# Where the products of a two-step graph walk stand: factoring x U1 + R (x U1') out of the first step

## The chip, the core and the metric

The kernel runs on one core of one Trainium2 chip. The metric is device time in microseconds (us) of one execution. The core's engines are called PE (matrix products), PEld (its weight loads), DVE (vector), ACT (scalar), POOL (GpSimd) and SP (which here issues DMAs).

## The reference

x has 2708 rows of 256 numbers, adj is a sparse 2708 x 2708 matrix. Layer 0 walks twice over two matrices and adds up terms; layer 1 is a graph attention over adj. Cut to what the change touches:

```
R = adj + I;  R = R / R.sum(-1)
Xf = X;  Xa = X;  Z = 0
for n in range(2):
    A  = top_p_attention(Xa)        # softmax of a bilinear form, smallest 10% dropped, rows sum to 1
    Xf = R @ Xf
    Xa = A @ Xa
    Z  = Z + Xf @ U1[n].T + Xa @ U2[n].T
h = X + Z
x = layernorm(x + (layernorm(h) * ln_g + ln_b))
x = layernorm(x + gat(x, adj))      # layer 1
```

The walk's part of Z is R x U1[0].T + R R x U1[1].T. It does not depend on the attention's part, apart from the sum.

## The kernel before, in words

The 2708 rows are cut into 22 tiles: 16 of 128 rows and 6 of 110. All products are in float32; one product shows as two records in the trace.

For each step s and tile t there are two streams of work. **The search** (`scores`, `survey`, `bound`, `candidates`, `settle`) computes a tile of exponentials e, 128 x 2708, finds the threshold of the top 90% and sets the rest to zero. It uses PE for the scores (L620), ACT for exponentials (L624) and, in step 1, four passes over e (L645), DVE for maxima (L725, L743), replacing (L745, L791) and masked products (L710, L794), and POOL for small numbers. **The attention product** (`weigh`) transposes e in six groups (L202), ACT copies each to SBUF as eT (L208), and PE multiplies 22 times (L217) with the values x (step 0) or ba (step 1). A search is begun three tiles ahead.

**The walk** is the third stream, a generator `walks()`. For s = 0 tile t takes 22 products (L845) of blocks of adj transposed (`blk`, loaded by SP into three buffers, two loads a tile) with xe, which is x with a column of ones; the sum lands in a PSUM tile `walk` of a pool with one buffer. `after_walk0` adds the tile's own row on DVE (xf, L858), takes the reciprocal of the row sum, transposes xf on PE (L603), and `terms1` multiplies by U1 of both steps at once (L890). ACT scales the two halves by the reciprocal: cs is the contribution of step 0, and yw = (R x) U1[1].T is the operand of the second walk. POOL adds the own row's share and x to cs (L900 to L902) and stores it in DRAM as c1. For s = 1 the walk multiplies with yw; `finish` scales the result on ACT (xw, L924), adds c1, c2 (the attention's share of step 0, from `terms2`, L910) and the attention of step 1 (`held`), makes both layer norms and calls `sources`, which prepares layer 1.

The order on PE, ACT, DVE and POOL is written out by hand, as the program emits it. `slot(spend)` moves every running search by one piece, then every running follow-up (`doing`), then emits `spend` walk products, fewer where a walk tile ends. A slot follows each of the six groups of an attention tile; the tuples SPEND_0 and SPEND_1 give its walk products. Ahead of step 0 there are ten slots (SPEND_FIRST), between the steps some sixteen (SPEND_BETWEEN). The second walk can't start before the last `after_walk0` is through (`unfinished`). SP's queue and the pools' buffers are ordered by the framework.

```
SPEND_FIRST, SPEND_0 = 5, (2, 2, 2, 2, 2, 1)
SPEND_BETWEEN, SPEND_1 = 6, (5, 5, 4, 5, 5, 4)
```

Of the kernel before, what the change touches and what calls it, by code (L numbers as in the profile page):

```python
# [8 lines left out]
F32 = mybir.dt.float32  # L9
BF16 = mybir.dt.bfloat16  # L10
I32 = mybir.dt.int32
AF = mybir.ActivationFunctionType
ALU = mybir.AluOpType
# [3 lines left out]
P = 128  # L17
# [3 lines left out]
CHUNK = 512  # L21
# [12 lines left out]
NARROW = 26.0  # L34


SPEND_FIRST, SPEND_0 = 5, (2, 2, 2, 2, 2, 1)
SPEND_BETWEEN, SPEND_1 = 6, (5, 5, 4, 5, 5, 4)
HELD = 8
LN2 = 0.6931471805599453  # L40

Z_LOW, Z_HIGH = 1e-25, 1e30
# [3 lines left out]
def kernel(  # L46
# [16 lines left out]
    nc = tc.nc  # L63
    N, D = x.shape
# [50 lines left out]
    vd = [kept.tile([P, D], F32, name=f"v_{t}") for t in range(NT)]  # L115
    bad = const.tile([1, 1], I32, name="bad")

    def load_x():
        step = 4
        for t0 in range(0, NT, step):  # L120
            by_tile(xe[:, t0:, 0:D], x, t0, min(t0 + step, NT))

    def layernorm(dst, src, m):

# [100 lines left out]
    def general_layer0():  # L225
        with ExitStack() as l0:
# [5 lines left out]
            u_sb = w0.tile([P, STEPS, 2, DC, D], F32, name="u_sb")  # L232
            g_sb = w0.tile([P, D], F32, name="g_sb")
            b_sb = w0.tile([P, D], F32, name="b_sb")
            load_x()
            nc.scalar.dma_start(w1_sb, w1T.rearrange("(c p) e -> p c e", p=P))
            nc.scalar.dma_start(w3_sb, w3T.rearrange("(c p) e -> p c e", p=P))
            for s in range(STEPS):
# [245 lines left out]
    def fast_layer0(ep, adjp):  # L484
# [32 lines left out]
            nc.scalar.dma_start(w2_sb[:, h, :], w2T)  # L517
        for h in range(2):
            nc.scalar.dma_start(wk_sb[:, :, h, :], w3T.rearrange("(c p) e -> p c e", p=P))
        load_x()  # L520
        for s in range(STEPS):
            for k, u in enumerate((u1T, u2T)):
                nc.scalar.dma_start(u_sb[:, k, :, s], u[s].rearrange("(c p) e -> p c e", p=P))
# [27 lines left out]
        nc.gpsimd.memset(wants, 0.0)  # L551
        nc.gpsimd.memset(haves, 0.0)

        yw = keep.tile([P, NT, D], F32, name="yw")
        ba = keep.tile([P, NT, D], F32, name="ba")
        rinv = keep.tile([P, NT], F32, name="rinv")
        qT = keep.tile([P, N], F32, name="qT")
# [1 line left out]
        dram = l0.enter_context(tc.tile_pool(name="dram", bufs=1, space=bass.MemoryType.DRAM))  # L559
        c1 = [dram.tile([P, D], F32, name=f"c1_{t}") for t in range(NT)]  # L560
        c2 = [dram.tile([P, D], F32, name=f"c2_{t}") for t in range(NT)]


        kT = [wk.tile([P, HN], F32, name="junk"), keep.tile([P, HN], F32, name="kT1")]
# [248 lines left out]
        def walks():  # L813

            queue = [
                (s, t, j0, j1)
                for s in range(STEPS) for t in range(NT) for j0, j1 in ((0, HT), (HT, NT))  # L820
            ]

            def load(s, t, j0, j1):
                m = rows[t]
                blk = adjp.tile([P, NT - HT, P], F32, name="blk")
                by_tile(blk[:, :, :m], adjT[:, off[t] : off[t + 1]], j0, j1)
                return blk

            ahead = load(*queue[0])
            for n, (s, t, j0, j1) in enumerate(queue):  # L830
                m = rows[t]
                cur, w = (xe, D + 1) if s == 0 else (yw, D)
                while s and unfinished:
                    yield True
                blk = ahead
                if n + 1 < len(queue):
                    ahead = load(*queue[n + 1])
                if j0 == 0:
                    ac = ps_wk.tile([P, CHUNK], F32, name="walk")
                    if s:  # L840
                        ca, cb = (finp.tile([P, D], F32, name=k) for k in ("ca", "cb"))
                        nc.sync.dma_start(ca[:m], c1[t][:m])
                        nc.sync.dma_start(cb[:m], c2[t][:m])
                for j in range(j0, j1):
                    nc.tensor.matmul(  # L845
                        ac[:m, :w], blk[: rows[j], j - j0, :m], cur[: rows[j], j, 0:w],
                        start=(j == 0), stop=(j == NT - 1),
                    )
                    if j == NT - 1:
                        doing.append(after_walk0(t, ac) if s == 0 else finish(t, ac, ca, cb))  # L850
                        next(doing[-1])
                    yield j == NT - 1

        def after_walk0(t, ac):
            m = rows[t]
            unfinished.add(t)
            xf = rowp.tile([P, D + 1], F32, name="xf")
            nc.vector.tensor_add(xf[:m], ac[:m, : D + 1], xe[:m, t, :])  # L858
            nc.vector.reciprocal(rinv[:m, t : t + 1], xf[:m, D : D + 1])
            yield  # L860
            tp = ps_tr.tile([P, 4, P], F32, name="tr")
            xT = turn(xf, m, tp, nc.scalar.copy)
            yield
            terms1(t, xT)
            unfinished.remove(t)

        pair = []
# [17 lines left out]
        def terms1(t, xT):  # L885

            m = rows[t]
            cy = ps_tr.tile([P, 4, P], F32, name="tr").rearrange("p a b -> p (a b)")
            for c in range(DC):
                nc.tensor.matmul(  # L890
                    cy[:m], xT[:, c, :m], u_sb[:, 0, c].rearrange("p s e -> p (s e)"),
                    start=(c == 0), stop=(c == DC - 1),
                )
            r = rinv[:m, t : t + 1]
            cs = rowp.tile([P, D], F32, name="cs")
            nc.scalar.activation(cs[:m], cy[:m, 0:D], AF.Copy, scale=r)
            nc.scalar.activation(yw[:m, t, :], cy[:m, D : 2 * D], AF.Copy, scale=r)

            own = rowp.tile([P, D], F32, name="own", bufs=1)
            nc.gpsimd.tensor_scalar(own[:m], yw[:m, t, :], r, None, op0=ALU.mult)  # L900
            nc.gpsimd.tensor_add(cs[:m], cs[:m], own[:m])
            nc.gpsimd.tensor_add(cs[:m], cs[:m], xe[:m, t, 0:D])  # L902
            nc.gpsimd.dma_start(c1[t][:m], cs[:m])

        def terms2(t, xT):
# [13 lines left out]
        def finish(t, ac, ca, cb):  # L919

            m = rows[t]
            xt = xe[:m, t, 0:D]
            xw = rowp.tile([P, D], F32, name="xw")[:m]
            nc.scalar.activation(xw, ac[:m, :D], AF.Copy, scale=rinv[:m, t : t + 1])  # L924
            yield
            while t not in held:
                yield
            hh = heldp.tile([P, D], F32, name="hh", bufs=4)[:m]
            nc.gpsimd.tensor_add(ca[:m], ca[:m], cb[:m])
            nc.gpsimd.tensor_add(ca[:m], ca[:m], held.pop(t)[:m])  # L930
            nc.gpsimd.tensor_add(hh, ca[:m], xw)
            yield
            for last in range(2):
                st, mv = small.tile([P, 6], F32, name="ln_st")[:m], small.tile([P, 2], F32, name="ln_mv")[:m]
                nc.vector.bn_stats(st, hh)
                nc.vector.bn_aggr(mv, st)
                yield
                yield
                ve, rs = new("ln_ve", m), new("ln_rs", m)
                nc.gpsimd.tensor_scalar(ve, mv[:, 1:2], LN_EPS, None, op0=ALU.add)  # L940
                nc.gpsimd.tensor_tensor(rs, ve, minus_half[:m], op=ALU.pow)
                yield
                yield
                nc.vector.tensor_scalar(
                    xt if last else hh, hh, mv[:, 0:1], rs, op0=ALU.subtract, op1=ALU.mult
                )
                yield
                yield
                if not last:
                    nc.gpsimd.tensor_mul(hh, hh, g_sb[:m])  # L950
                    nc.gpsimd.tensor_add(hh, hh, b_sb[:m])
                    nc.gpsimd.tensor_add(hh, hh, xt)
                    yield
                    yield
            yield from sources(t, rowp, ps_tr)


        engines = {nc.tensor.engine, nc.scalar.engine, nc.vector.engine, nc.gpsimd.engine}
        going, doing, unfinished = [], [], set()
        ready, held = {}, {}  # L960
        stream = walks()
        owed = [0]
# [30 lines left out]
        def step(s, cur, spend):  # L993
            for t in range(NT):
# [6 lines left out]
                def between(n):  # L1001
                    last = n == len(groups) - 1
                    if last:
                        xa = heldp.tile([P, D], F32, name="xa1")
                        nc.scalar.activation(xa[:m], ac[:m, :D], AF.Copy, scale=rden)
                        if s:
                            held[t] = xa
                        else:
                            doing.append(after_attention0(t, xa))
                    slot(spend[n], (s, t + 3) if last else None)  # L1010
# [25 lines left out]
                    )  # L1036


        for grp in groups:
            k = rows[grp[0]]  # L1040
            w, c0 = k * len(grp), off[grp[0]]
            tp = ps_lg.tile([P, 2, CHUNK], F32, name="lg")
            for c in range(DC):
                for q, t in enumerate(grp):
                    nc.tensor.transpose(
                        tp[:, c, q * k : (q + 1) * k], xe[:k, t, c * P : (c + 1) * P],
                        ident[:k, :k],
                    )
            e = ep.tile([P, N], F32, name="e")
            xT = e[:, 0 : DC * CHUNK].rearrange("p (c n) -> p c n", c=DC)  # L1050
            nc.scalar.copy(xT[:, 0, :w], tp[:, 0, :w])
            nc.vector.tensor_copy(xT[:, 1, :w], tp[:, 1, :w])
            pj = ps_lg.tile([P, 2, CHUNK], F32, name="lg")
            for n, wm in enumerate((wq, wk_sb)):
                for c in range(DC):
# [5 lines left out]
            keep_k(0, c0, w, pj[:, 1], nc.vector.tensor_copy)  # L1061
        with tc.manual_schedule(engines=engines):
            for n in range(10):
                slot(SPEND_FIRST if n else 0, (0, n // 4) if n in (0, 4, 9) else None)
            layer1_weights()
            step(0, xe, SPEND_0)
            while doing:
                slot(SPEND_BETWEEN)

# [242 lines left out]
```

## Time and profile before

| what | value |
|---|---|
| median of 3 runs | 1678.13 us (1677.03 to 1678.82) |
| the profiled execution | 1677.58 us, span 1675.8 us |
| PE busy | 1610.0 us, 96% of the span |
| PEld, DVE, ACT, POOL busy | 1058.0, 1217.0, 766.8, 423.4 us |
| walk products with xe, with yw (L845) | 240.5 and 228.1 us |
| attention products with x, with ba (L217) | 233.3 and 234.1 us |
| transposes of e (L202) | 140.8 us |
| U1 products (L890), transposes of xf (L603) | 42.9 and 9.1 us |

Busy times of PE overlap with each other, since products are pipelined. In the lines of the trace the form is start, duration, engine, line, operation, out<-in and, in brackets, the idle time of the engine before it with what ended it; in the chain of waits it is start, duration, engine, tile and line.

### The profile page before, as it was taken

The page shows a single profiled execution, that of the slowest core. Times are in us where ns is not written, and L with a number is a line of the kernel's source. Part 1 is how long each engine was busy: PE and PEld are TensorE (multiplying, and loading weights), DVE is VectorE, ACT ScalarE, POOL GpSimd, SP SyncE. Part 2 cuts the span into 40 slices and gives each one's busy share as a digit, 9 for nine tenths or more (in the row PEclk, how much of TensorE's full clock was granted, in tenths as well). Part 3 has the DMA queues.
Part 4 walks back from the last instruction along what each step waited for, and adds up shares of the span by engine and source line. Part 5 has one row for each costly group of instructions (what it writes and reads, how often), then busy time and mean ns, then how long its engine had stood idle before and what let it go on. Part 6 is the DMA issues. An engine that isn't in the chain of part 4 may idle for free.

```text
span 1675.8 us, 23985 instructions
## 1 busy us (share of the span) xinstructions
PE 1610.0 (96%) x8218; PEld 1058.0 (63%) x8218; DVE 1217.0 (73%) x3660; ACT 766.8 (46%) x1324; POOL 423.4 (25%) x893
## 2 busy tenths in 40 slices
PE   7999999999999999999999999999997999999895
PEld 4677777777777776777787878777785222322332
DVE  2954554565455019888999999998994899888886
ACT  1333333333333255656576666667555334243231
POOL 0310111111011023223244444444434020420313
PEclk9999999999999999999999999999999999999998
DMA  6211011111110142212322322323222332232231
GB/s 166 73 47 46 26 43 40 40 31 40 40 43 25 43 104 67 63 49 73 79 72 79 87 68 82 89 58 77 72 65 88 98 99 86 88 93 77 76 86 39
DMA packets 153873, 113.89 MB, mean 68 GB/s; under 512 B 39898, under 2 KB 144094, under 8 KB 153742
## 3 DMA queue, kind: packets, MB, share of 16 engines
q1 hardware_dynamic: 149278, 105.18, 23.4%
q0 software_dynamic: 2112, 5.55, 1.0%
q10 hardware_dynamic: 2352, 1.54, 0.3%
q8 instruction: 67, 1.10, 0.3%
q14 instruction: 64, 0.52, 0.1%
HBM read 101.16 MB, written 11.09 MB: 67 GB/s over the span
## 4 chain that ended last, share of the span: by engine, by line
PE 78%; DVE 9%; ACT 5%; POOL 4%; issue 3%; DMA 0%; ACTq 0%; POOLq 0%; DVEq 0%; SPq 0%
PE att L217 23%; PE walk L845 19%; PE acc L1233 12%; PE acc L1240 6%; PE lg L620 5%; PE tr L202 4%; ACT e L624 3%; PE tr L910 2%; PE tr L890 2%; PE lg L1056 1%; PE tr L591 1%; DVE cand L725 1%; ACT eT L208 1%; DVE scr L791 1%; POOL res L1192 1%
## 5 line engine op out<-in xcount | busy, mean ns | idle before, releaser
L645 ACT ACTIVATE junk<-e,minus,rth 128x2708 bf16<-128x2708 f32 (+1 forms) x88 | 232.8, 2646 | 35.7 <-POOL rth L677 34.6
L845 PE MATMUL walk<-xe,blk 128*128 128x257 f32 (+3 forms) x968 | 240.5, 382 | 0.0
L217 PE MATMUL att<-ba,eT 128*128 128x256 f32 (+3 forms) x968 | 234.1, 383 | 5.0 <-ACT eT L208 5.0
L217 PE MATMUL att<-xe,eT 128*128 128x256 f32 (+3 forms) x968 | 233.3, 381 | 4.3 <-ACT eT L208 4.3
L208 ACT COPY eT<-tr 128x512 f32<-128x512 f32 (+5 forms) x264 | 138.2, 537 | 206.3 <-PE tr L202 206.1
L1233 PE MATMUL acc<-pt,v 128*64 128x512 f32 (+3 forms) x1056 | 226.0, 550 | 4.7 <-DVE pt L1225 3.8
L845 PE MATMUL walk<-yw,blk 128*128 128x256 f32 (+3 forms) x968 | 228.1, 381 | 1.7 <-ACT xw L924 1.7
L725 DVE MAX8 cand<-e 128x8 f32<-128x170 f32 (+1 forms) x352 | 89.2, 322 | 178.8 <-ACT e L624 178.8
L845 PEld LDWEIGHTS walk<-xe,blk 128*128 128x128 f32 (+3 forms) x968 | 174.6, 186 | 54.2 <-issue 29.3
L845 PEld LDWEIGHTS walk<-yw,blk 128*128 128x128 f32 (+3 forms) x968 | 176.7, 186 | 41.5 <-issue 11.5
L1225 DVE SCALAR_TENSOR_TENSOR pt<-e,tj,blk 128x1024 f32<-128x1024 f32 (+3 forms) x176 | 185.8, 1115 | 19.8 <-issue 8.0
L217 PEld LDWEIGHTS att<-ba,eT 128*128 128x128 f32 (+3 forms) x968 | 171.4, 186 | 32.7 <-ACT eT L208 10.0
L217 PEld LDWEIGHTS att<-xe,eT 128*128 128x128 f32 (+3 forms) x968 | 170.9, 186 | 30.9 <-ACT eT L208 7.2
L624 ACT ACTIVATE e<-lg 128x1024 f32<-128x1024 f32 (+1 forms) x132 | 121.1, 921 | 132.3 <-PE lg L620 132.3
L1233 PEld LDWEIGHTS acc<-pt,v 128*64 128x64 f32 (+1 forms) x1056 | 72.1, 137 | 153.5 <-issue 112.3
L202 PE MATMUL tr<-ident,e 128*128 128x128 f32 (+3 forms) x968 | 140.8, 270 | 4.6 <-ACT xT L606 3.8
L202 PEld LDWEIGHTS tr<-ident,e 128*128 128x128 f32 (+3 forms) x968 | 115.1, 139 | 32.3 <-ACT xT L606 6.1
L1165 ACT ACTIVATE blk<-blk 128x1024 f32<-128x1024 f32 (+3 forms) x66 | 63.2, 958 | 155.3 <-DMA blk<-in_adjT_dram 136.3
L1240 PE MATMUL acc<-pt,sb 128*32 128x512 f32 (+3 forms) x1056 | 124.5, 549 | 0.0
L1225 DVE SCALAR_TENSOR_TENSOR pt<-r,tj,blk 128x1024 f32<-128x1024 f32 (+1 forms) x88 | 109.8, 1306 | 10.8 <-issue 7.0
L631 POOL TENSOR_TENSOR fact<-zp 128x1 f32<-128x1 f32 (+1 forms) x44 | 24.8, 563 | 359.0 <-ACT e L624 349.1
L725 DVE MAX8 cand<-scr 128x8 f32<-128x97 f32 (+1 forms) x616 | 101.9, 243 | 0.0
(203 smaller groups left out, 1999.6 us busy)
## 6 DMA issues: line engine op xcount, KB each, us to landing
blk<-in_adjT_dram SPq DMA_DIRECT2D x32, 704.0 KB
blk<-in_adjT_dram SPq DMA_DIRECT2D x32, 512.0 KB
blk<-in_adjT_dram SPq DMA_DIRECT2D x48, 330.0 KB
blk<-in_adjT_dram SPq DMA_DIRECT2D x32, 320.0 KB
blk<-in_adjT_dram SPq DMA_DIRECT2D x12, 605.0 KB
blk<-in_adjT_dram SPq DMA_DIRECT2D x12, 440.0 KB
blk<-in_adjT_dram SPq DMA_DIRECT2D x18, 283.6 KB
c<-cs POOLq DMA_DIRECT2D x32, 128.0 KB, 2.1
```

Of the source, the lines that this page charges most:

```text
L202: nc.tensor.transpose(tr[: rows[t], q, :m], e[:m, off[t] : off[t + 1]], ident[:m, :m])
L208: copy(eT[:k, : len(grp), :m], tr[:k, : len(grp), :m])
L217: nc.tensor.matmul(acc, eT[: rows[t], q, :m], value(t), start=(t == 0), stop=(t == NT - 1),)
L620: nc.tensor.matmul(lg[:m, h, :w], qT[part, cols], kT[s][part, c0 : c0 + w], start=True, stop=True,)
L624: nc.scalar.activation(halves[:m, :, c0 : c0 + w], lg[:m, :, :w], AF.Exp, accum_out=zp[:m, n : n + 1],)
L645: nc.scalar.activation(junk[:m], e[:m], func, scale=rth, bias=minus1[:m], accum_out=acc)
L725: nc.vector.max(cand[:, n, :], src[:m, n * size : min(N, (n + 1) * size)])
L845: nc.tensor.matmul(ac[:m, :w], blk[: rows[j], j - j0, :m], cur[: rows[j], j, 0:w], start=(j == 0), stop=(j == NT - 1),)
L1165: nc.scalar.activation(bar, bar, AF.Sign)
L1225: nc.vector.scalar_tensor_tensor(pt[:k, :gw], r[h // 2][:k, h % 2, :gw], tj[:k, j, h : h + 1], mask, op0=ALU.max, op1=ALU.mult,)
L1233: nc.tensor.matmul(acc[h // 2][c][q * FO : (q + 1) * FO, :w], v[j][:k, h - 1 + q, :], pts[h - 1 + q][:k, c0 : c0 + w], **at,)
L1240: nc.tensor.matmul(acc[2][c][h * 32 : (h + 1) * 32, :w], sb[:k, j, h : h + 1].to_broadcast([k, 32]), pts[h][:k, c0 : c0 + w], **at,)
```

## The change

The walk's part is factored as R (x U1[0].T + R (x U1[1].T)). x is multiplied by both U1 ahead of step 0, in the first ten slots, from the transposed x that the projections of step 0 have made anyway and which is now kept (in ba, which is free until step 0 writes it). The second half takes the place of x in xe; the first goes to DRAM as c1. x itself lies in xm. The first walk multiplies with xe as before; `after_walk0` then scales by the reciprocal and adds c1, and the result overwrites xm, the operand of the second walk. So no first walk can end before step 0's attention has used x: all walk products are emitted between the steps and in step 1. `terms1` no longer scales or adds; `finish` reads x back from the input, adds the own row on DVE and scales on ACT. Since the second walk comes late in step 1, the attention's result of step 1 is stored in DRAM (c3) for the first 18 tiles and loaded again. The layer norms of `finish` have two pauses (`yield`) fewer in each of the two rounds.

```
-SPEND_FIRST, SPEND_0 = 5, (2, 2, 2, 2, 2, 1)
-SPEND_BETWEEN, SPEND_1 = 6, (5, 5, 4, 5, 5, 4)
-HELD = 8
+SPEND_BETWEEN, SPEND_1 = 7, (7, 6, 7, 7, 6, 7)
+HELD, WAITING = 6, 4
...
-        yw = keep.tile([P, NT, D], F32, name="yw")
+        xm = keep.tile([P, NT, D], F32, name="xm")
+        load_x(xm)
...
-                cur, w = (xe, D + 1) if s == 0 else (yw, D)
+                cur, w = (xe, D + 1) if s == 0 else (xm, D)
...
+                    ca = finp.tile([P, D], F32, name="ca", bufs=4)
                     if s:
-                        ca, cb = (finp.tile([P, D], F32, name=k) for k in ("ca", "cb"))
+                        cb = finp.tile([P, D], F32, name="cb")
+                        nc.sync.dma_start(ca[:m], x[off[t] : off[t + 1], :])
+                        nc.sync.dma_start(cb[:m], c2[t][:m])
+                        if t in c3:
+                            held[t] = finp.tile([P, D], F32, name="cc")
+                            nc.sync.dma_start(held[t][:m], c3[t][:m])
+                    else:
                         nc.sync.dma_start(ca[:m], c1[t][:m])
-                        nc.sync.dma_start(cb[:m], c2[t][:m])
...
         def after_walk0(t, ac, ca):
             xf = rowp.tile([P, D + 1], F32, name="xf")
             nc.vector.tensor_add(xf[:m], ac[:m, : D + 1], xe[:m, t, :])
-            nc.vector.reciprocal(rinv[:m, t : t + 1], xf[:m, D : D + 1])
+            nc.vector.reciprocal(r, xf[:m, D : D + 1])
             yield
-            tp = ps_tr.tile([P, 4, P], F32, name="tr")
-            xT = turn(xf, m, tp, nc.scalar.copy)
-            yield
-            terms1(t, xT)
+            nc.gpsimd.tensor_scalar(xf[:m, :D], xf[:m, :D], r, None, op0=ALU.mult)
+            nc.gpsimd.tensor_add(xm[:m, t, :], xf[:m, :D], ca[:m])
...
             cs = rowp.tile([P, D], F32, name="cs")
-            nc.scalar.activation(cs[:m], cy[:m, 0:D], AF.Copy, scale=r)
-            nc.scalar.activation(yw[:m, t, :], cy[:m, D : 2 * D], AF.Copy, scale=r)
-            own = rowp.tile([P, D], F32, name="own", bufs=1)
-            nc.gpsimd.tensor_scalar(own[:m], yw[:m, t, :], r, None, op0=ALU.mult)
-            nc.gpsimd.tensor_add(cs[:m], cs[:m], own[:m])
-            nc.gpsimd.tensor_add(cs[:m], cs[:m], xe[:m, t, 0:D])
+            nc.scalar.copy(cs[:m], cy[:m, 0:D])
+            nc.scalar.copy(xe[:m, t, 0:D], cy[:m, D : 2 * D])
             nc.gpsimd.dma_start(c1[t][:m], cs[:m])
...
         def finish(t, ac, ca, cb):
-            nc.scalar.activation(xw, ac[:m, :D], AF.Copy, scale=rinv[:m, t : t + 1])
+            nc.vector.tensor_add(xw, ac[:m, :D], xm[:m, t, :])
             yield
+            nc.scalar.activation(xw, xw, AF.Copy, scale=rinv[:m, t : t + 1])
...
-                        if s:
+                        if s and t in c3:
+                            nc.gpsimd.dma_start(c3[t][:m], xa[:m])
+                            stored.add(t)
+                        elif s:
                             held[t] = xa
...
             for n in range(10):
-                slot(SPEND_FIRST if n else 0, (0, n // 4) if n in (0, 4, 9) else None)
+                slot(0, (0, n // 4) if n in (0, 4, 9) else None)
+                for t in range(n * NT // 10, (n + 1) * NT // 10):
+                    terms1(t, x_turned[:, :, off[t] : off[t + 1]])
             layer1_weights()
-            step(0, xe, SPEND_0)
+            step(0, xm, [0] * len(groups))
```

## The prediction

> **What bounds the kernel now.** I read the page's slices first, then the busy times by stretch, then the chain of waits inside single tiles. PE has a 9 nearly everywhere until layer 1; DVE is half idle in step 0 and close to full in step 1:
>
> ```profile
> PE   7999999999999999999999999999997999999895
> ...
> DVE  2954554565455019888999999998994899888886
> ```
>
> The stretches, cut at the first score of step 0, its first transpose of e, its last product, the first transpose of step 1 and its last product (columns: stretch, length, then busy time of PE, PEld, DVE, ACT, POOL, clock, DMA):
>
> ```profile
> 40.30:70.50 30.20, 29.39 (x128) 19.92 (x128) 26.33 (x95) 9.46 (x20) 10.01 (x12) 1.00 0.28 73
> 70.50:587.90 517.40, 509.58 (x2443) 376.91 (x2442) 261.66 (x959) 171.94 (x386) 56.66 (x126) 1.00 0.14 39
> 587.90:653.70 65.80, 62.51 (x267) 43.84 (x265) 28.04 (x106) 36.01 (x51) 21.01 (x49) 1.00 0.38 98
> 653.70:1280.00 626.30, 615.25 (x3027) 482.67 (x3026) 562.38 (x2097) 402.30 (x659) 244.52 (x550) 1.00 0.27 70
> ```
>
> PE is 98% busy in both steps, DVE 51% in step 0 and 90% in step 1. So moving walk products from step 0 to step 1 is no gain in itself: both stretches are PE's. What counts is PE work removed, and cover. A full tile of step 0 (the chain of waits, 284 to 300 us) shows the one place where PE is not the chain:
>
> ```profile
> 284.16 1.08 PE lg L620 x4
> 285.25 0.02 issue
> 285.27 2.12 ACT e L624 x4
> 287.39 0.48 ACT eT L208
> 287.88 0.04 issue
> 287.92 2.00 PE att L217 x8
> ...
> 291.04 0.87 PE walk L845 x4
> 291.91 0.44 PE tr L202 x4
> 292.35 1.73 PE att L217 x8
> ```
>
> At the head of a tile the chain is scores, two exponentials, copy of eT. The one walk product put there (the last entry of SPEND_0) lies beside ACT and is free. The other slots pay 0.87 us for two products (x4 records; a product is two records), 0.435 each.
>
> **The skill.** "Perfetto Trace Analysis", Identifying the Most-Contended Engine, says that matmul busy share is a poor measure of how near PE is to its limit. The trace agrees: 98% busy includes those heads. I count products times their spacing instead. The same page, Matmuls, wants independent groups to rotate through PSUM banks so that a drain overlaps the next group; the walk has one bank (ps_wk), and PE waited only 1.7 us for its drain in step 1 (ACT xw L924). "GPSIMD Engine Reference", 8. Key points, says that GpSimd can't access PSUM and shares its SBUF interfaces with VectorE. Here POOL reads SBUF only, and its add at L951 took 0.73 us alone but 1.85 us at 1288.18 beside pt (L1225).
>
> **The change, part by part.** The instruction order of the changed kernel gives the counts; durations are of the profiled run.
>
> Products are conserved: 968 walks. Before: 44 in the first stretch, 242 in step 0, 97 between, 585 in step 1. After: 0, 0, 110, 858. Likewise 22 pairs of U1 products (L890, 4 records of 0.43: 1.72 us): before 1, 11, 4, 6; after all 22 in the first stretch. Gone are the 44 transposes of xf (L603), 0.28 us a pair, with waits for xf and xT.
>
> 1. First stretch: 21 pairs in, 36.1; 44 walks out, 19.1; a transposition pair out, 0.3. **+16.7 us.** ACT's 22 x 0.74 us of copies fit beside 38 us of PE, and so do POOL's 22 issues of c1 stores (0.65 each), which move along. SP's first walk blocks and c1 loads are behind the loads of x, with 500 us to spare.
> 2. Step 0: ten walks per tile outside the head, 220 x 0.435 = 95.7; the three tiles without a new search get their head walk back too, 1.3; 11 U1 pairs, 18.9; 11 xf turns. Adjoining tiles took 22.28 us (no U1 pair, no projection) and 26.09; taking 4.35, 1.72 and the projection's 1.73 from the latter leaves 0.36 for a turn, 4.0 in all. **-119.9 us.** The other 19 head walks (8.3 us of work) go away without shortening anything, and cost full price later: their cover is lost. Next late at the head is again ACT's eT. Per tile DVE has 262/22 = 11.9 us in 17.9 to 19.7: no bound.
> 3. Between: 4 pairs and 6 turns out, 6.9 + 1.7, and waits for xf and xT, 2.8 + 0.3; 13 walks in, 5.6. Then the first search of step 1 has to be done when PE arrives. Its operations from the first score, without POOL's L900 to L903, which stood in its way before: exponentials done at 4.4, POOL's first guess 2.0, four tallies of 2.85 with 2.4 of POOL between them, bound 4.9, candidates 4.7, settle 6.2 and 3.1, mask 3.75, product 3.1, two drains of 0.6: 47.4 us. PE takes 89 walks, 38.7, and 16 score products, 8.0: 46.7. I take 0.8 us of wait (0 to 4). **-5.3 us.**
> 4. Step 1: 273 walks in, 118.5 (0.434); 6 pairs and 5 turns out, 10.3 + 1.4; in the last tile PE waited 0.86 for e and 3.28 for total (L1125), which now is placed later, -4.1; +1.3 for one drain there. **+104.0 us.** I leave the rest of a tile as it was: 28.83 us on average for 28 products and 0.9 of sources, so a tile will take 32.5, then 34.5.
> 5. Layer 1: 24 of 32 transposes for the second targets, before in an idle PE behind step 1, now stand in the PE-bound layer 1, 24 x 0.11. **+2.6 us.**
>
> Sum: 16.7 - 119.9 - 5.3 + 104.0 + 2.6 = **-1.9 us** against the profiled run's 1677.58 (span 1675.8 and 1.8 around it), which is 0.55 below the median: 1676 us.
>
> Costed at nothing: POOL loses L900 to L902 (2.4 us a tile) and gets a scale and an add (1.7) and 18 stores of c3 (0.65), in a step where it is 39% busy. SP gets 22 loads of x and 18 of c3, queued between the walk blocks; SP already waited 82 us for cb (L843 on POOL), and PE waited for no block, since three are held. The 7.5 MB more are 12 GB/s beside 70. If that cover went, PE would stand before a walk. ACT loses a copy per tile. DVE gets 0.43 us per finish.
>
> **An added wait that the trace shows only in part.** The bank of step 1's second walk is now emptied by DVE (xw plus xm), not ACT, and all 22 first-walk drains but those between also fall into step 1: 39 drains on DVE, behind the search's operations, with PE's next walk behind them. The drains of before in step 1, and one late one between:
>
> ```profile
> 649.12 0.42 DVE L858 TENSOR_TENSOR xf<-walk,xe 110x257 f32<-110x257 f32 x1
> ...
> 649.59 0.41 PE L603 MATMUL tr<-ident,xf 110*128 110x110 f32 x2 [1.79 <-DVE xf L858]
> ...
> 669.70 0.43 DVE L858 TENSOR_TENSOR xf<-walk,xe 110x257 f32<-110x257 f32 x1 [0.96 <-PE walk L845]
> ...
> 694.46 0.43 DVE L858 TENSOR_TENSOR xf<-walk,xe 110x257 f32<-110x257 f32 x1 [4.54 <-PE walk L845]
> ```
>
> In step 1 DVE stood waiting for the walk; once, between, PE waited 1.79. Bounds: 0, or 39 x 1.8 = 70 us; below nothing is excluded, as PE waited 1.7 for ACT at most. After a walk a transpose group and a product group (2.2 us) cover the drain, and DVE will have some 25 to 28 us of work in 32 to 35. I take 0 and keep 20 us for the range.
>
> **Rivals.**
> - Forecast, no change to speak of, 1671 to 1681: chance 0.50.
> - DVE's drains decide (slower): where DVE runs more than 2.2 us behind PE, PE's next walk waits. DVE's burst of e times mask (3.05) and bound (5) speaks for it, the idle times above against it. 13 of 39 at 1.8 us: +23, 1699; from two drains on it eats the -1.9. Chance 0.18.
> - The stores of c1 bound the first stretch (slower): cs has two buffers; copy 0.37, issue 0.65, landing 2.1 is 3.1 us for two tiles against PE's 3.44, but with the longest landing, 3.3, it is 4.3, or 0.43 us a tile over: +9.5, 1686. Chance 0.12.
> - Step 1 gains from a DVE with slack (faster): the chain of waits runs through DVE from 1185 to 1262 us, to the last e. If 0.3 us a tile (the 28.83 over the 28.5 of pure PE) vanishes and the last sources come earlier, -6 and -4: 1666. Chance 0.20.
> - That the walks don't leave step 0: excluded, the order has none there.
>
> **How the numbers follow.** A measurement tells about 0.2%, 3.4 us. Faster by more: the fourth case and three tenths of the forecast, 0.34. Slower: the second and third and a little of the forecast, 0.31. Within: 0.35. The forecast's own range is 1671 to 1681; the range that holds 8 in 10 goes to 1665 and 1689.
>
> **What would show it.** Right: step 0 near 398 us with no walk and heads still 3.8 us from score to product; first stretch near 47; step 1 near 730 with PE at 98% and DVE under 80%; no wait of the walk for xw. Wrong: PE walk waiting for DVE xw or xf in step 1 by more than 5 us; ACT cs waiting for a DMA in the first stretch; a wait for blk.

## The result, and the profile after

The changed kernel takes 1672.94 us (median of 4, 1672.26 to 1673.97); the kernel before takes 1678.08 us beside it. The ratio is 0.997, with a 95% interval of 0.9953 to 0.9988: a small gain, 5.1 us. The forecast was 1676 us, 1.9 us less than before, with 1671 to 1681 as its range; the range held.

The slices of the page, busy tenths of PE and DVE, show where things went. PE is nearly as before. DVE has a slice with next to nothing to do where step 0 ends (the twelfth, 459 to 501 us), and in step 1 it stands at 7 to 9 tenths, where it stood at 8 and, mostly, 9:

```profile
PE   7999999999999999999999999999998999999895
...
DVE  2766666667605877877788988978883989888886
```

The stretches of the changed kernel are cut at the same events as those before (columns: stretch, length, busy time of PE, PEld, DVE, ACT, POOL with counts, clock, DMA share, GB/s). In order: first scores to the first transpose of e, step 0, between the steps, step 1, from the last attention product to layer 1's first product, layer 1:

```profile
39.56:85.54 45.98, 45.98 (x121) 18.67 (x121) 30.40 (x107) 22.00 (x59) 13.16 (x27) 1.00 0.21 68
85.54:483.82 398.28, 380.55 (x1891) 276.98 (x1889) 249.75 (x920) 154.95 (x355) 25.71 (x84) 1.00 0.03 9
483.82:546.29 62.47, 60.08 (x267) 46.15 (x268) 28.57 (x110) 32.80 (x40) 15.17 (x42) 1.00 0.42 110
546.29:1271.05 724.76, 718.84 (x3532) 578.22 (x3530) 581.29 (x2140) 394.85 (x630) 274.75 (x582) 1.00 0.35 92
1271.05:1287.09 16.04, 8.66 (x46) 5.71 (x44) 9.94 (x16) 8.27 (x41) 6.91 (x11) 0.89 0.55 156
1287.09:1670.40 383.31, 358.69 (x2226) 113.11 (x2226) 319.67 (x375) 132.89 (x166) 77.17 (x110) 0.97 0.29 83
```

The last two stretches of the kernel before, which the prediction doesn't show, were:

```profile
1279.84:1298.14 18.30, 11.42 (x64) 8.19 (x62) 11.32 (x16) 10.82 (x46) 11.25 (x14) 0.91 0.55 165
1298.14:1675.80 377.66, 352.61 (x2202) 110.31 (x2202) 318.35 (x374) 129.00 (x152) 77.90 (x110) 0.98 0.29 82
```

The differences in the lengths are +15.8, -119.0, -3.5, +98.7, -2.3 and +5.7 us. The time ahead of the first scores was 40.3 us and is 39.6; it lay between 39.6 and 41.3 in all runs here, so this -0.7 is taken for no effect of the change. With it the sum is -5.4, the difference of the two spans (1670.4 and 1675.8).

In step 0 PE is busy for 380.55 of 398.28 us: 17.7 us of stops, where there were 7.8. The list of waits of PE in step 0 (sum in us, how many, the longest) names them:

```profile
PE att L216 <- ACT eT L207: 17.4, 21, 0.9
```

A head of a tile there, as the timeline of PE shows it (start, duration, operation, in brackets the idle time before it), has nothing between the transposes and the first attention group:

```profile
287.26 1.99 PE L621 MATMUL lg<-junk,qT 64*128 64x512 f32 x8
289.18 1.09 PE L201 MATMUL tr<-ident,e 128*128 128x128 f32 x8
291.15 1.99 PE L216 MATMUL att<-xm,eT 128*128 128x256 f32 x8 [0.87 <-ACT eT L207]
```

From the first score to the attention group it is 3.89 us. Before it was 3.83 with a walk product there, and 4.1 in the heads that held a turn of xf too (a turn is the two transposes of xf): ACT's two exponentials and its copy set it, with or without one walk product on PE.

In step 1 the list of waits holds no walk product at all, so DVE's drains were covered:

```profile
PE att L216 <- ACT eT L207: 5.3, 22, 0.3
PE tr L201 <- DVE e L795: 0.5, 1, 0.5
```

### The profile page after: what moved, and what is told of

Read it like the earlier page. It is cut to its first block, busy times and chain, and to the rows that moved or that the text cites. A ratio compares the mean times of both kernels' runs of the same rounds, so it can differ in the third digit from the quotient of the medians.

```text
span 1670.4 us, 24116 instructions
## 1 busy us (share of the span) xinstructions
PE 1601.4 (96%) x8174; PEld 1054.8 (63%) x8174; DVE 1228.5 (74%) x3682; ACT 753.0 (45%) x1302; POOL 414.9 (25%) x889
## 5 line engine op out<-in xcount | busy, mean ns | idle before, releaser
L216 PE MATMUL att<-xm,eT 128*128 128x256 f32 (+3 forms) x968 | 229.3, 381 | 17.4 <-ACT eT L207 17.4
L853 PE MATMUL walk<-xe,blk 128*128 128x257 f32 (+3 forms) x968 | 223.8, 382 | 1.9 <-DVE xf L867 1.8
L853 PE MATMUL walk<-xm,blk 128*128 128x256 f32 (+3 forms) x968 | 221.8, 380 | 0.0
L216 PEld LDWEIGHTS att<-xm,eT 128*128 128x128 f32 (+3 forms) x968 | 171.2, 186 | 44.7 <-ACT eT L207 22.2
L853 PEld LDWEIGHTS walk<-xm,blk 128*128 128x128 f32 (+3 forms) x968 | 177.6, 186 | 32.7 <-issue 4.9
L867 DVE TENSOR_TENSOR xf<-walk,xe 128x257 f32<-128x257 f32 (+1 forms) x22 | 9.4, 426 | 113.9 <-PE walk L853 113.9
```

The source lines that it names most:

```text
L216: nc.tensor.matmul(acc, eT[: rows[t], q, :m], value(t), start=(t == 0), stop=(t == NT - 1),)
L853: nc.tensor.matmul(ac[:m, :w], blk[: rows[j], j - j0, :m], cur[: rows[j], j, 0:w], start=(j == 0), stop=(j == NT - 1),)
```

## The experiments

Ratios are to the kernel before on the same chip (1677.2 to 1677.8 us in the three sets of runs).

**Products in the heads of step 0.** What is the lost cover worth? The products by U2 of earlier tiles (`terms2`) go there.

```
                 ahead = turned(n + 1)
+            if head and n == 0:
+                head()
...
+        def head():
+            if late:
+                terms2(*late.pop(0))
...
-            terms2(t, xT)
+            if t < NT - 2:
+                late.append((t, xT))
+            else:
+                terms2(t, xT)
```

> The changed kernel, with the U2 products of step 0 (terms2, two products of 0.86 us a tile) taken out of the slots and put into the heads of later tiles, between the second group of transposes and the first attention group, with the idle walk bank as their place in PSUM; only the last two tiles keep them where they were. Theory (cover lost at the heads): PE stood 17.4 us in step 0 for the copy eT at 21 heads, 0.8 to 0.9 us at each of the 19 with a new search; 1.72 us of products put there fills all of it. Twenty of them leave the slots, 34.4 us, and come back at the heads for 34.4 less the idle time: step 0 goes from 398 us to about 381 to 383, the whole to 1656 to 1658 us (0.990 to 0.991 of the kernel before's 1678 becomes about 0.987). Rival (the head is bound by something else, as scores or the copy of the next group): the idle time only moves to the second attention group, and the time stays within 3 us of 1673.

Measured: 1651.54 us, ratio 0.984 (0.9827 to 0.9854). Step 0 in the stretches, and a head in PE's timeline:

```profile
86.42:462.99 376.57, 375.40 (x1891) 276.31 (x1889) 247.89 (x920) 156.72 (x355) 25.86 (x84) 1.00 0.03 9
```

```profile
136.64 1.09 PE L201 MATMUL tr<-ident,e 128*128 128x128 f32 x8
137.57 1.88 PE L921 MATMUL walk<-u_sb,xT 128*128 128x512 f32 x4
139.29 1.89 PE L218 MATMUL att<-xm,eT 128*128 128x256 f32 x8
```

The stop is gone, and the time is below the theory's 1656 to 1658 us. Step 0 is 21.7 us shorter, more than the 17.4 us of stops: with the same products, PE's busy time fell by 5.2 us too (380.55 to 375.40). Taken from start to start, less the listed idle time, 3.2 us of it are in the transposes ahead of the stop and 2.0 in the attention products behind it. So a stop cost 0.26 us beyond its idle time (5.2 over 20 stops). The moved products also use another bank, the idle one of the walk; that explains little, since PE waited only 0.3 us in step 0 of the changed kernel for the bank that they left. The first stretch, the one between the steps and step 1 are as in the changed kernel, within 0.1 us.

**The kernel before without its head product.** Was it free, as the prediction had it?

```
-SPEND_FIRST, SPEND_0 = 5, (2, 2, 2, 2, 2, 1)
+SPEND_FIRST, SPEND_0 = 5, (2, 2, 2, 2, 2, 0)
...
-SPEND_BETWEEN, SPEND_1 = 6, (5, 5, 4, 5, 5, 4)
+SPEND_BETWEEN, SPEND_1 = 6, (5, 5, 5, 5, 5, 4)
```

> The kernel before with SPEND_0 = (2, 2, 2, 2, 2, 0) and SPEND_1 = (5, 5, 5, 5, 5, 4): nothing but the 22 walk products at the heads of step 0 go to step 1. Theory (a product at a head is free, anywhere else it costs 0.434 us): step 0 gets only the three uncovered ones back, -1.3; step 1 pays 22 x 0.434 = 9.5; in all +8.2, 1686 us, and PE's waits for eT in step 0 go from 4.3 to about 12.5 us. Rival (step 1 has slack for them, since PE waits there for DVE and ACT): within 2 us of 1678.

Measured: 1684.33 us, ratio 1.0034 (1.0021 to 1.0048): +6.5 us, 3.5 to 8.1 by the interval. PE's waits in step 0, first in the kernel before, then here:

```profile
PE att L217 <- ACT eT L208: 4.3, 13, 0.4
PE tr L202 <- ACT xT L606: 3.6, 9, 0.4
```

```profile
PE att L217 <- ACT eT L208: 14.6, 19, 0.9
PE tr L202 <- ACT yw L897: 1.0, 2, 0.6
PE tr L202 <- ACT xT L606: 0.4, 1, 0.4
```

The first theory's mechanism holds: a head without a product takes 3.82 us from the first score to the attention group, one with a product took 3.83, so the product there was free. The total is 1.7 us below the theory's. One thing that the theory left out is of that size: the turns of xf now fall at other places, mostly outside the heads, and the waits of PE's transposes for a bank that ACT empties (xT and yw) went from 3.6 to 1.4 us. This was read from the traces, not tried alone.

**DVE's drains four times over.**

```
-            nc.vector.tensor_add(xf[:m], ac[:m, : D + 1], xe[:m, t, :])
+            for _ in range(4):
+                nc.vector.tensor_add(xf[:m], ac[:m, : D + 1], xe[:m, t, :])
...
-            nc.vector.tensor_add(xw, ac[:m, :D], xm[:m, t, :])
+            for _ in range(4):
+                nc.vector.tensor_add(xw, ac[:m, :D], xm[:m, t, :])
```

> The changed kernel with each of DVE's 44 additions that empty the walk bank (xf and xw) written four times over, same operands and same result, so that the bank comes free 1.3 us later and DVE has 57 us more work. Forecast's step (2.2 us of transposes and products of attention cover the drain): in step 1 next to nothing, 0 to 5 us; between the steps two or three drains at 1.3 us, 2 to 4; in all 1675 to 1682 us. Rival (the drains decide, DVE runs behind PE): each of 39 drains in step 1 costs 1.3 us, 1720 us, or with DVE at 88% busy about half of it, 1695 us.

Measured: 1695.45 us, ratio 1.0109 (1.0093 to 1.0124), 22.5 us more than the changed kernel. Of these, 7.1 lie between the steps (69.53 for 62.47 us, where 2 to 4 were expected) and 14.1 in step 1 (738.89 for 724.76), where PE now waits:

```profile
PE walk L853 <- DVE xw L927: 6.5, 5, 1.9
PE att L216 <- ACT eT L207: 5.3, 22, 0.3
PE tr L201 <- DVE e L795: 1.8, 1, 1.8
```

The total is the rival's lower number, but not its place: it put all of it into step 1. There the added 1.3 us at 39 drains are 51 us, of which 14 came through, more than the 0 to 5 of the forecast. The waits listed grew by 7.8 us; of the rest, some 3.4 us (an estimate) go with two times of 3.4 us, from 888.3 and 1267.1 us on, in which the granted clock was 0.5, while it was 1.0 all through step 1 of the changed kernel. The cover is real, but it has not 1.3 us to spare everywhere: drains don't decide in the changed kernel, and would if they were somewhat later.

**The pauses put back.**

```
                 nc.vector.bn_aggr(mv, st)
                 yield
+                yield
...
                 nc.gpsimd.tensor_tensor(rs, ve, minus_half[:m], op=ALU.pow)
                 yield
+                yield
```

> The changed kernel with the two pauses (yield) of finish's layer norms put back, as in the kernel before. Theory: they only matter at the end of step 1, where the last tiles' layer norms and sources stand before layer 1; two pauses in each of two rounds push the sources of the last tiles behind the last attention product, and the stretch between the last product and layer 1's first one grows by 0 to 4 us: 1673 to 1677 us. Rival (the earlier operations on DVE and POOL without pauses made the gain of the change): 1678 us or more. Other rival (fewer pauses made DVE wait for POOL, which costs): 1670 us.

Measured: 1677.74 us, ratio 0.9999 (0.999 to 1.0007). The whole gain of the change is gone. Step 1, the stretch behind it and layer 1:

```profile
546.84:1272.29 725.45, 717.82 (x3524) 577.23 (x3522) 574.82 (x2139) 392.63 (x621) 280.10 (x577) 1.00 0.35 92
1272.29:1292.06 19.77, 10.51 (x53) 6.92 (x51) 12.38 (x18) 9.83 (x50) 10.91 (x16) 0.81 0.55 156
1292.06:1675.10 383.04, 358.41 (x2226) 113.11 (x2226) 318.78 (x374) 132.82 (x166) 77.30 (x110) 0.97 0.28 82
```

Behind the last attention product it takes 19.77 us with the pauses and 16.04 without; step 1 differs by 0.7, with one wait of 1.1 us for xw. So the theory had the place right and the size too small (4.8 for 0 to 4), and the rival had the total: with the pauses as before, the factoring and all that it moves gain nothing that can be measured (-0.1 us, -1.7 to +1.2 by the interval).

**The pauses taken out of the kernel before**, the same edit the other way round.

> The kernel before with the two pauses in each round of finish's layer norms taken out, and nothing else. Theory (the pauses lengthen the end of step 1 in either kernel; putting them back into the changed kernel cost 4.8 us, 3.7 of it between the last attention product and layer 1): the same here, less what moves of the transposes for the second targets into layer 1, so 1673 to 1676 us, and 14 to 15 us between the last product and layer 1 in place of 18.3. Rival (the pauses only matter where the second walk ends late, as in the changed kernel): 1677 to 1679 us.

Measured: 1678.08 us, ratio 1.0001 (0.9993 to 1.0009). The rival's number, not for its reason. Step 1, the stretch behind it and layer 1:

```profile
653.24:1280.71 627.47, 616.60 (x3028) 483.62 (x3027) 565.40 (x2098) 401.40 (x660) 260.92 (x553) 0.99 0.26 70
1280.71:1296.67 15.96, 9.99 (x49) 7.56 (x48) 9.79 (x14) 8.13 (x37) 6.80 (x11) 0.81 0.57 169
1296.67:1677.40 380.73, 356.07 (x2215) 111.90 (x2214) 318.86 (x374) 131.08 (x160) 78.29 (x110) 0.97 0.28 83
```

The stretch behind the last product shrinks here too, from 18.3 to 16.0 us. But PE has 2215 products in layer 1 where it had 2202: 12 of the 32 transposes for the second targets have moved there, and layer 1 takes 3.1 us more; step 1 takes 1.4 more. In the changed kernel it is 2226 with the pauses and without, 24 transposes, so there the gain was kept. That this displacement is the whole cause was read from the traces, not isolated. What the two runs show together is that neither half gains alone: the pauses taken out of the kernel before bring nothing, the factoring with its pauses brings nothing, and both at once bring 5.1 us.

**The turns put back.** What does the factoring save on PE?

```
             nc.vector.reciprocal(r, xf[:m, D : D + 1])
             yield
+            turn(xf, m, ps_tr.tile([P, 4, P], F32, name="tr"), nc.scalar.copy)
+            yield
```

> The changed kernel with the two transposes of xf on PE and the copy of their result on ACT put back into after_walk0, one pause later as in the kernel before; the copy is not read by anything. It prices what the factoring saves on PE. Theory (22 turns at 0.28 us, and PE's next transposes wait now and then for the bank that ACT empties, 3.6 us in step 0 of the kernel before): +6.2 to +10, 1679 to 1683 us. Rival (transposes hide in PE's other waits): 1673 us.

Measured: 1678.33 us, 5.4 us more than the changed kernel, ratio 1.0001 (0.9993 to 1.001). The first theory, a little under its lower end. The 18 turns in step 1 take 4.1 us by the starts, 0.23 each and not 0.28, without a wait for the bank. In the profiled run 3.3 us are in step 1 and 0.5 between the steps; 2.0 are in layer 1. Of these 1.8 lie behind the last operation of DVE, where PE has nothing left to do: from there to the end of the span it is 8.2 us, in the changed kernel 6.5, in the other runs 6.4 to 7.0. I know no reason for it. So the turns explain some 3.8 of the 5.4 us. The edit also puts a pause back into `after_walk0`, which was not tried alone.

**A second product at the heads of the kernel before.**

```
-SPEND_FIRST, SPEND_0 = 5, (2, 2, 2, 2, 2, 1)
+SPEND_FIRST, SPEND_0 = 5, (2, 2, 2, 2, 1, 2)
```

> The kernel before with SPEND_0 = (2, 2, 2, 2, 1, 2): one walk product of each tile of step 0 is moved from the fifth slot to the head, where one stands already. Theory (a stop of PE at the head costs its idle time and some 0.26 us more to run empty and fill again, as the heads filled with U2 products showed: 21.7 us for 16.5 us of idle time): 4.2 us of idle time in 13 heads and 13 x 0.26: -6 to -8, 1670 to 1672 us. Rival (only the listed idle time can be had): -3 to -4, 1674 to 1675 us. Third (the head pays each product in full): 1678 us.

Measured: 1675.79 us, ratio 0.9988 (0.9982 to 0.9995), -1.9 us: none of the three. A head in PE's timeline:

```profile
284.15 1.14 PE L845 MATMUL walk<-xe,blk 128*128 128x257 f32 x4
285.13 1.04 PE L202 MATMUL tr<-ident,e 128*128 128x128 f32 x8
286.46 2.00 PE L217 MATMUL att<-xe,eT 128*128 128x256 f32 x8 [0.29 <-ACT eT L208]
```

The two products stand ahead of the transposes. ACT was through with the exponentials at 285.5 and then waited itself, for the first of these transposes, as its timeline shows:

```profile
285.82 1.07 ACT L208 COPY eT<-tr 128x512 f32<-128x512 f32 x2 [0.29 <-PE tr L202]
```

The head has two chains, ACT's exponentials and PE's transposes; both end in the copy eT. Work ahead of the transposes covers the first and lengthens the second. One product fits: 3.83 us with it, 3.82 without. The second does not: a head with two takes 4.22 us, so that 0.39 of its 0.434 us is paid, as the third expectation had it. Only every second head holds two, since at the others a walk tile ends behind the first.

So filling the stop is not what gained 1.9 us. In step 0 the waits for eT even rose, from 4.3 to 6.9 us. What fell are the waits for xT, from 3.6 us to none, since the turns of xf no longer stand in the heads. That too was read from the traces only.

**The same two products behind the transposes.**

```
+    def more():
+        owed[0] += 2
+        while owed[0] > 0 and not ended[0]:
+            owed[0] -= 1
+            ended[0] = next(stream, True)
...
-SPEND_FIRST, SPEND_0 = 5, (2, 2, 2, 2, 2, 1)
+SPEND_FIRST, SPEND_0 = 5, (2, 2, 2, 2, 1, 0)
```

> The kernel before with two walk products of each tile of step 0 at the head, behind the second group of transposes in place of one ahead of the first, taken from the fifth slot as when two stood ahead (1675.8 us); where a walk tile has just ended they stay owed. Theory (a product ahead of the transposes delays the transpose that ACT's copy eT needs, so that the head keeps a stop of 0.3 us for the copy; behind them it fills just this stop): the 6.9 us of waits for eT go, with what a stop costs beyond its idle time, -6 to -9 against 1675.8: 1667 to 1670 us. Rival (the place at the head makes no difference): 1674 to 1676 us.

Measured: 1672.33 us, ratio 0.997 (0.9958 to 0.9982), 3.5 us less than with the products ahead (3.0 by the two ratios, as the chips differ): between the theory and the rival. A head in PE's timeline, then PE's waits in step 0 and a little around it:

```profile
283.17 1.99 PE L622 MATMUL lg<-junk,qT 64*128 64x512 f32 x8
285.09 1.09 PE L202 MATMUL tr<-ident,e 128*128 128x128 f32 x8
286.02 1.03 PE L847 MATMUL walk<-xe,blk 128*128 128x257 f32 x4
287.00 2.00 PE L219 MATMUL att<-xe,eT 128*128 128x256 f32 x8
```

```profile
PE tr L202 <- ACT yw L899: 5.2, 10, 0.6
PE att L219 <- ACT eT L208: 0.2, 1, 0.2
```

Two products behind the transposes fit where two ahead of them did not: this head takes 3.83 us and not 4.22. The waits for eT fall from 6.9 to 0.2 us, as the theory said. A new wait of 5.2 us took the rest: at every second head a pair of U1 products now stands ahead of the transposes, and these wait for the bank that ACT empties of it (yw).

**Heads of both steps filled.** In step 1, three of the seven walk products of the last slot are emitted at the head.

```
-SPEND_BETWEEN, SPEND_1 = 7, (7, 6, 7, 7, 6, 7)
+SPEND_BETWEEN, SPEND_1, FILL = 7, (7, 6, 7, 7, 6, 4), 3
...
+    def more():
+        for _ in range(FILL):
+            if next(stream, True):
+                break
```

> The changed kernel with the U2 products in the heads of step 0, as in the first experiment, and in step 1 three walk products of each tile moved from the slot just ahead of the next tile's first transposes to just behind its second group of transposes, ahead of the first attention group. Theory (each stop of PE costs its idle time and about 0.26 us more): 22 heads of step 1 at 0.25 + 0.26 us, -11 us against the first experiment, 1640 us. Rival (only the listed 5.6 us can be had): 1646 us. Other rival (the three products come later before DVE has emptied the bank, or the next tile's e is late, and the gain is lost): 1651 us.

Measured: 1661.73 us, ratio 0.9909 (0.9896 to 0.9923), 10 us worse than the first experiment. The other rival holds, and it is worse than it said (1651 us). Step 1's waits:

```profile
PE walk L855 <- DVE xw L935: 10.2, 3, 5.2
PE walk L855 <- DVE xf L869: 5.2, 2, 3.0
```

All five stand at one kind of place, of which this is one, in PE's timeline:

```profile
852.87 0.70 PE L855 MATMUL walk<-xm,blk 110*128 110x256 f32 x2
853.41 1.04 PE L201 MATMUL tr<-ident,e 128*128 128x128 f32 x8
856.72 1.56 PE L855 MATMUL walk<-xm,blk 128*128 128x256 f32 x6 [2.27 <-DVE xw L935]
```

The product at 852.87 ends a walk tile, and the head opens the next one after a single block of transposes. The bank must be empty by then, and DVE is behind with the search, as its timeline shows:

```profile
852.89 3.04 DVE L713 SCALAR_TENSOR_TENSOR scr<-e,hi 128x2708 f32<-128x2708 f32 x1
856.25 0.42 DVE L935 TENSOR_TENSOR xw<-walk,xm 128x256 f32<-128x256 f32 x1
```

At all five places DVE is in this pass over e, and its drain begins 2.6 to 5.8 us after the walk tile's last product.

**Filled, but not across the end of a walk tile.**

```
     def more():
-        for _ in range(FILL):
-            if next(stream, True):
-                break
+        owed[0] += FILL
+        while owed[0] > 0 and not ended[0]:
+            owed[0] -= 1
+            ended[0] = next(stream, True)
```

> As the kernel with products in the heads of both steps, but the products at a head of step 1 are only emitted where no walk tile has just ended; otherwise they stay owed and follow in the next slot. Theory (all five waits of 15.5 us for xf and xw there stood at a head that opened a new walk tile, with 0.93 us of transposes as the only cover of DVE's drain): these waits go, the 5.6 us of waits for eT stay away, and with what a stop costs beyond its idle time step 1 takes some 9 us less than in the first experiment: 1642 to 1645 us. Rival (the products come too late for DVE all over, whatever the head): 1655 to 1662 us.

Measured: 1646.61 us, ratio 0.9814 (0.9801 to 0.9828): 30.6 us faster than the kernel before and about 26 faster than the changed one, a little short of the theory's 1642 to 1645. Step 1 and its waits:

```profile
526.28:1245.47 719.19, 715.60 (x3535) 578.33 (x3534) 577.55 (x2142) 396.58 (x638) 275.83 (x582) 1.00 0.34 93
```

```profile
PE walk L855 <- DVE xw L935: 1.4, 2, 0.8
PE tr L201 <- DVE e L797: 1.2, 2, 0.9
PE att L218 <- ACT eT L207: 1.0, 4, 0.2
```

Step 1 is 5.6 us shorter than in the first experiment, not 9; some stops for drains and for e stay. Of the 5.6, 2.4 are idle time (5.94 less 3.59) and 3.2 busy time: stops again cost more than they show. This kernel beats both.

## Why the prediction was right, point by point

The time was inside the range and on the right side, but the agreement is better than the reasons. Most of the signs named for it came: step 0 at 398.3 us with heads of 3.89, the first stretch at 46.0, step 1 at 724.8 without a wait for xw; DVE stood at 80% there, not under it. Still, the sum had no term for what made the gain (see below), and its own errors offset each other in part: step 1 came out 5.3 us shorter than forecast, the stretch between the steps and the end of the kernel 2.6 us longer. That the range held is luck to that extent.

1. **First stretch.** +16.7 forecast, +15.8 measured. PE is busy in all of its 45.98 us. The rival of the c1 stores is out: no copy of ACT waited for a store, and the stores landed in 2.0 to 2.6 us.
2. **Step 0.** -119.9 forecast, -119.0 measured. That 19 products at the heads go "away without shortening anything" and "their cover is lost" was the right mechanism: heads took 3.83 us with a product, 3.82 without, and here 3.8 to 3.9. Taking them out of the kernel before cost 6.5 us (8.1 at most by the interval) where this reckoning gives 8.2; that the waits for xT would fall along with them was no part of it.
3. **Between.** -5.3 forecast, -3.5 measured. The search was no wait: e was ready. (The pieces listed for it add to 47.2 us, not 47.4, which changes nothing.) Against it, the wait for xf, which I took out, came back as PE's walk waiting for DVE's xf (1.8 us in two waits) and a transpose waiting for xa (0.6).
4. **Step 1.** +104.0 forecast, +98.7 measured, the largest miss. Walk products took 118.8 us more by the starts (118.5 forecast), U1 products and turns 11.6 less (11.7). The idle time fell by 5.1, not by 2.8: besides the 3.3 us for total, the 1.7 us for ACT's xw are gone, and the 1.3 us allowed for a drain didn't come. The other 3.4 us are 1.7 in the attention products' spacing, with their number unchanged, and small groups at the end. DVE stands at 80% of the stretch.
5. **Layer 1.** +2.6 forecast for 24 transposes. Layer 1 takes 5.7 us more and the stretch ahead of it 2.3 less, +3.4. In layer 1 three blocks of eight transposes take 3.2 us by the starts, 0.13 each. Some 1.7 us more (an estimate) are in its first 3.4 us, in which the granted clock was 0.5: 8 records of PE fell into them, where as long a time at the full clock took 16 in the kernel before. First the changed kernel, then the one before:

```profile
1287.09:1290.49 3.40, 3.40 (x8) 1.00 (x10) 2.89 (x3) 1.63 (x3) 0.00 (x0) 0.50 0.87 274
```

```profile
1298.14:1301.50 3.36, 3.36 (x16) 1.23 (x16) 1.47 (x2) 2.45 (x4) 0.00 (x0) 1.00 0.64 168
```

In the kernel before, such a time (1288.6 to 1292.0 us) was over before layer 1 began. The last 0.8 of the 5.7 I can't place.

**The step that is missing** is the pauses. The sum had no term for the two removed `yield` lines (four pauses a tile, as there are two rounds); only the fourth rival touched their effect, with 4 us for earlier last sources. Putting them back cost 4.8 us. With them the change is 1677.74 against 1677.84 us, which is the forecast's "no change to speak of". So the forecast of the rest was near, -1.9 against about 0, and there too by errors that offset each other: with the pauses, step 1 grew by 99.4 us for the 104.0 of the forecast, the end of the kernel by 6.9 for 2.6. The measured gain needs the pauses gone, which the sum didn't have. But it isn't theirs alone: in the kernel before, taking them out gained nothing.

**The rivals.** The drains do not decide here: no walk product waited in step 1. But the run with longer drains and the one with earlier walk tiles show how near they are. Whether the cover of "2.2 us" is enough depends on how late DVE comes. In the changed kernel, at 1211 us, 0.86 us of PE's work between two walk tiles were enough, as DVE's drain began at once. The Trainium skill's "Perfetto Trace Analysis", section Matmuls, asks for groups to rotate through banks for just this; with one walk bank, the order has to supply the distance. These runs put a number on it: 0.9 to 1.0 us of transposes was too little at five heads where DVE came 2.6 to 5.8 us late, and PE stood for 2.2 to 5.2 us at each. A gain in step 1 from a slacker DVE is not shown: what ended are waits for ACT's xw, whose drain moved to DVE, and for total, which is placed later, and tiles did not get shorter throughout.

**Where the factoring's saving went.** This is for the change with the pauses put back, and a rough account. Saved: the turns, some 3.8 us (the run with them put back, less the 1.8 us behind the last operation), and the waits of before that went, 3.6 and 0.5 for xT, 3.3 for total and 1.7 for xw, some 9 us by the trace. Given back: the heads' cover, 6.5 (the run without head products), and by the stretches 5.4 in layer 1 (383.04 against 377.66) and 1.5 ahead of it (19.77 against 18.30). That is 13 against 13; but the 6.5 are already net of 2.1 us of the waits for xT, so it doesn't close better than some 2 us. The turns and the cover were tried, the rest is read from the traces.

## What to carry to other kernels

When work leaves a stage, ask which of it lay beside another engine's chain: that part comes back at full price elsewhere, and something else should take its place. Filler belongs behind the instructions that the other engine waits for and ahead of the one that waits for it. It must not open a bank anew before the bank's drain is sure to be through. Cost every line of a diff, the harmless-looking pauses too: here neither the factoring nor the removal of the pauses gained anything alone, and both together gained 5.1 us. And when a filler moves, look at what else moves with it: in three runs here waits for another bank came or went by 2 to 5 us.

## What the runs showed that I had not expected

A stop of PE costs more than its idle time: filling 20 stops brought 0.26 us each on top, in the groups on both sides. A stop that seems to be the other engine's fault can be PE's own: with two products ahead of the transposes, ACT waited 0.29 us for PE, and then PE 0.29 us for ACT.
